# A transformer block on one core: when the turn of the softmax maxima and the copies of the scores are emitted

## The chip, the core and the metric

The kernel runs on one core of one Trainium2 chip. A core has a matrix engine (TensorE, PE in the profile; PEld are its weight loads), a vector engine (VectorE, DVE), a scalar engine for activations and copies (ScalarE, ACT), a general engine (GpSimd, POOL) and SyncE (SP), which issues most of the DMAs. Each has its own queue of instructions, and they wait for each other by semaphores. Matrix products end in PSUM, a small accumulation memory; all else lies in SBUF. The metric is the device time of one execution, in microseconds (us).

## What is computed

One block, float32 throughout: layer norm, attention with 32 heads of width 32, residual, layer norm, gated feed-forward network, residual, on x of shape (2, 1024, 1024).

```python
def _L0_attn_ref(x, attn_qkvw, attn_qkvb, attn_ow, attn_ob):
    qkv = x @ attn_qkvw + attn_qkvb
    ...
    scores = jnp.einsum('bhqd,bhkd->bhqk', q, k) * scale
    probs = jax.nn.softmax(scores, axis=-1)
    ctx = jnp.einsum('bhqk,bhkd->bhqd', probs, v)
    ctx = jnp.transpose(ctx, (0, 2, 1, 3)).reshape(B, S, H)
    return ctx @ attn_ow + attn_ob
...
    up = xt @ W_up.T
    gate = jax.nn.silu(xt @ W_gate.T)
    y = gate * up @ W_down.T
...
x = x + _L0_attn_ref(_layernorm(x, axis=-1), ...)
x = x + _L0_ffn_ref(_layernorm(x, axis=-1), ...)
```

W_gate and W_up are 2752 x 1024.

## The kernel before

**Units.** Attention is cut into 64 units: two batches, two blocks of 512 queries each, and 16 pairs of heads. Units are numbered 0 to 63 in that order; units 0 to 15 are the first phase. A unit has eight key tiles of 128 keys. The scores of one key tile, for both heads, are a PSUM tile `s` of 128 x 1024 (keys down, heads and queries across); there are two such tiles. `scores(i)` makes the key tiles 2i and 2i+1 with four small matmuls (L510). Each is then read twice: VectorE keeps a running maximum over the key tiles in `top` (L528), and ScalarE copies the scores to SBUF, `p` (L529). For key tile 0 VectorE copies it instead (L524), and the maximum of key tile 1 starts from that copy. Within `take`, which does both for one key tile, the maximum is emitted first and the copy right behind it.

**The maxima.** After key tile 7, `top` holds a maximum over eight keys for each partition and query, and it remains to take it over the 128 partitions. `maximum` does that in steps: VectorE transposes 32 x 32 blocks of half of `top` (L543) and reduces them into `part` (L544), the same for the other half, TensorE transposes `part` (L558, the instruction of `turn`, into one of the three PSUM tiles `lin` that all projections share), VectorE reduces once more, negated, to `neg` (L559). SyncE stores that in DRAM (L564) and loads it back spread over all partitions as `m` (L567).

**The exponentials.** `less_maximum` adds `m` to the copied scores (L574, on GpSimd; in the first phase key tiles 3 and 7 on VectorE), `exponential` is ScalarE's (L580), and `add` adds the exponentials of two key tiles (L590; on VectorE for key tiles 3 and 7, in the first phase for all four pairs, otherwise on GpSimd). `values` multiplies them with V, and their pair sums with ones for the softmax's divisor, into `acc` (L602). The copies live in a ring of `RING` buffers. The values of a unit lie in one of two buffers, which `load_v` fills by SyncE (L496).

**The rest.** The other work of TensorE is projections of q, k and v (L370, L432), the output projection (L764), gate and up products in a seven-product scheme (L906), and the down projection (L1047, L979). Their results leave the `lin` tiles by VectorE (L920 to L933, L1060, L776, L444) or ScalarE (L918, L384, L386).

**What sets the order.** The whole order is written out by an `Emitter`. It has a clock in ns, which advances by each step's cost in TensorE time (`MM4` = 855 for a full matmul of 512 columns). Steps come from two lists, a `fill` (projections and feed-forward) and a `paced` list (attention); the beats of the paced list are spread evenly over the cost of the list that they go with. There are eight beats to a unit, and even beats make scores. `later(delay, fn)` puts `fn` off until the clock has advanced by `delay`; when it is called, its instructions go to the end of their engines' queues. The numbers in the calls of `later` are thus places in the order, not times. `LAG` is the number of beats between the end of a unit's scores and its first `less_maximum`, beside a fixed eight; three beats later the values follow. `needs` and `gives` hold a step back until another is done in this clock, such as `("max", n)` for the subtractions of unit n.

Of the kernel before, what the change touches and what calls it, by code (L numbers as in the profile page):

```python
# [12 lines left out]
ALU = mybir.AluOpType  # L13
# [4 lines left out]
HD = 32  # L18
# [112 lines left out]
def preln_block_kernel(  # L131
# [14 lines left out]
    nc = tc.nc  # L146
# [13 lines left out]
    MM4, MM1 = 855.0, 230.0  # L160
    UNITS = HEADS // 2
    QTR = 4
    LAG = 2
    RUN = 4
    RING = NT + LAG + RUN + 4

# [27 lines left out]
    def Pt(name):  # L194
        return att.tile([P, S], F32, tag="p", bufs=RING, name=name)

    def lps(name, shape=(P, NH)):
        return psum.tile(list(shape), F32, tag="lin", bufs=3, name=name)

    def small(shape, tag, bufs, name):  # L200
        return const.tile(shape, F32, tag=tag, bufs=bufs, name=name)
# [27 lines left out]
    em = Emitter()  # L229
# [235 lines left out]
    class Unit:  # L465
# [35 lines left out]
        def scores(self, i):  # L501

            kts = (2 * i, 2 * i + 1)
            ps = [
                psum.tile([P, S], F32, tag="s", bufs=2, name=f"s_{self.name}_{kt}") for kt in kts
            ]
            for a in range(2):
                for h in range(2):
                    rows = slice((2 * a + h) * HD, (2 * a + h + 1) * HD)
                    nc.tensor.matmul(  # L510
                        ps[a][:, h * NH : (h + 1) * NH],
                        self.k[rows, i * P : (i + 1) * P],
                        self.q[rows, :],
                        start=True,
                        stop=True,
                    )


            for kt in kts:
                self.p[kt] = Pt(f"p_{self.name}_{kt}")  # L520

            def take(kt, s):
                if kt == 0:
                    nc.vector.tensor_copy(self.p[0], s)  # L524
                    return
                if kt == 1:
                    self.top = att.tile([P, S], F32, tag="top", bufs=1, name=f"top_{self.name}")
                nc.vector.tensor_tensor(self.top, s, self.p[0] if kt == 1 else self.top, ALU.max)  # L528
                nc.scalar.copy(self.p[kt], s)  # L529

            take(kts[0], ps[0])
            em.later(1700.0, lambda: take(kts[1], ps[1]))
            if kts[1] == NT - 1:
                self.maximum()

        def maximum(self):

            n = HD // NS
            self.m = att.tile([P, S], F32, tag="m", bufs=2, name=f"m_{self.name}")

            def half(s):
                cols = slice(s * NH, (s + 1) * NH)
                nc.vector.transpose(self.m[:, cols], self.top[:, cols])  # L543
                nc.vector.tensor_reduce(  # L544
                    part[:, s * n : (s + 1) * n],
                    self.m[:, cols].rearrange("p (b j) -> p b j", j=HD),
                    AX.X,
                    ALU.max,
                )

            for s in range(NS):
                em.later(4600.0 + 1800.0 * s, lambda s=s: half(s))
            d2 = dram.tile([S], F32, tag="d2", bufs=3, name=f"d2_{self.name}")
            neg = small([HD, HD], "neg", 1, f"neg_{self.name}")

            def turn():
                pt = lps(f"top_{self.name}", (P, P))
                nc.tensor.transpose(pt, part, ident)  # L558
                nc.vector.tensor_reduce(  # L559
                    neg, pt[:HD, :].rearrange("b (a i) -> b i a", i=HD), AX.X, ALU.max, negate=True  # L560
                )

            em.later(8600.0, turn)
            em.later(9600.0, lambda: nc.sync.dma_start(d2.rearrange("(b i) -> b i", i=HD), neg))  # L564
            em.later(
                12000.0,
                lambda: nc.sync.dma_start(self.m, d2.partition_broadcast(P)),  # L567
                ("max", self.n),
            )
# [62 lines left out]
    def attention_steps(cuts):  # L632
# [7 lines left out]
        def load_step(k, i):  # L640
            if k < len(units):
                q.add(lambda: units[k].load(i), needs=("qk", units[k].b, units[k].g))

        for i in range(2):
            load_step(0, i)
        for n in range(total + NT + LAG + 3):
            if n in cuts:
# [13 lines left out]
            else:  # L661
                q.add(lambda: None, beat=True)
            k, kt = divmod(n - NT - LAG, NT)
            if 0 <= k < len(units):
                if kt == 0:
                    q.add(units[k].differences)
                q.add(lambda k=k, kt=kt: units[k].less_maximum(kt), needs=("max", k))
            k, kt = divmod(n - NT - LAG - 3, NT)
            if 0 <= k < len(units) and kt % RUN == RUN - 1:
# [512 lines left out]
    with tc.manual_schedule():  # L1182
# [87 lines left out]
        keep = keep_qk  # L1270
        for (q, late), beats in zip(rests, [*lists[1:], None]):
            em.run(joined([keep, q]), beats, side=side)
            keep = late
# [53 lines left out]
```

## Time and profile before

| | |
|---|---|
| Median of 3 runs | 3360.42 us (3348.86 to 3375.26) |
| Profiled execution | 3347.63 us, span 3345.6 us |
| Mean granted clock of TensorE | 0.986 |
| Scores' first copy, L524 VectorE | 64 x 1223 ns |
| Scores' other copies, L529 ScalarE | 448 x 1012 ns |
| Maxima, L528 VectorE | 384 x 1222 ns, 64 x 1224 ns |
| Transposition and reduction of halves, L543, L544 | 128 x 701 ns, 128 x 686 ns |
| Transposition of `part`, L558 TensorE | 64 x 316 ns |
| Subtraction, L574 GpSimd | 480 x 2468 ns |
| Exponential, L580 ScalarE | 512 x 1057 ns |
| Addition of two exponentials, L590 | VectorE 160 x 1554 ns, GpSimd 96 x 2392 ns |

A line of the groups names the source line, the engine, what is written and read, shapes and count, then busy time, the mean of one, the idle time of the engine ahead of it, and what ended most of that. A line of the waits names who waited, for whom, then the total in us, the number of waits and the longest. In a timeline a row has its start and its length, the engine, line and operation, and in brackets the engine's idle time before it and what ended it. In the windows each engine's busy time is given with its number of instructions, then the granted clock of TensorE as a share of full speed, the DMA engines' share and GB/s.

### The profile page before, as it was taken

The numbers are of one execution on the slowest core, as the hardware profiler recorded it, in microseconds if no ns is written. First come the engines' busy times: TensorE is split into PE (matmuls) and PEld (weight loads), VectorE is DVE, ScalarE is ACT, GpSimd is POOL, SyncE is SP. The second block draws the span as 40 slices with busy tenths as digits, with TensorE's granted clock in tenths as the row PEclk, the third lists the DMA queues.
The fourth block names the chain that finished last, engine by engine and source line by source line (L and its number), as shares of the span: only waits on it lengthen the run. The fifth ranks groups of instructions, "written<-read, shape, count | busy, mean of one in ns | idle before, by whom it ended". The sixth has DMA issues, their size and how long they took to land.

```text
span 3345.6 us, 44180 instructions
## 1 busy us (share of the span) xinstructions
PE 3220.0 (96%) x16576; PEld 1819.2 (54%) x16576; DVE 1971.8 (59%) x2526; ACT 1375.1 (41%) x1506; POOL 1722.6 (51%) x839
## 2 busy tenths in 40 slices
PE   8999999999899999998999999989999999999999
PEld 4444444444346655663465556634655566476775
DVE  2366676664356666657566666665666664344434
ACT  2244554444355544453554545535544454010000
POOL 0267667775665555556755666567555555200000
PEclk9999999999999999999999999989999999999999
DMA  4566666663524454456344544463445444544552
GB/s 152 172 186 202 208 202 202 194 191 120 164 86 127 146 144 134 147 145 202 92 136 140 146 143 140 144 200 96 128 141 145 140 135 127 197 136 154 153 153 97
DMA packets 337251, 507.32 MB, mean 152 GB/s; under 512 B 105360, under 2 KB 122000, under 8 KB 337040
## 3 DMA queue, kind: packets, MB, share of 16 engines
q1 hardware_dynamic: 280848, 405.91, 40.1%
q10 hardware_dynamic: 56192, 98.60, 9.7%
q8 instruction: 132, 2.16, 0.3%
q14 instruction: 79, 0.65, 0.1%
HBM read 429.14 MB, written 75.24 MB: 151 GB/s over the span
## 4 chain that ended last, share of the span: by engine, by line
PE 81%; DVE 10%; DMA 3%; ACT 2%; issue 2%; POOL 1%; SPq 0%; ACTq 0%; DVEq 0%; POOLq 0%
PE p L906 27%; PE pq L370 11%; PE pd L1047 10%; PE acc L602 10%; PE s L510 7%; PE po L764 6%; PE pvv L432 6%; DVE top L528 2%; PE pd L979 1%; DVE x L1060 1%; DVE part L544 1%; DVE m L543 1%; DVE p L590 1%; PE pg L950 1%; POOL p L574 1%
## 5 line engine op out<-in xcount | busy, mean ns | idle before, releaser
L574 POOL TENSOR_TENSOR p<-p,m 128x1024 f32<-128x1024 f32 x480 | 1174.1, 2468 | 174.8 <-DMA m<-d 160.0
L529 ACT COPY p<-s 128x1024 f32<-128x1024 f32 x448 | 452.1, 1012 | 997.4 <-DVE top L528 959.6
L528 DVE TENSOR_TENSOR top<-s,top 128x1024 f32<-128x1024 f32 x384 | 469.1, 1222 | 397.1 <-PE s L510 380.6
L580 ACT ACTIVATE p<-p 128x1024 f32<-128x1024 f32 x512 | 530.4, 1057 | 262.3 <-POOL p L574 203.0
L906 PE MATMUL p<-sum,m 128*128 128x256 f32 x2688 | 616.3, 383 | 12.3 <-ACT gate L918 8.4
L906 PEld LDWEIGHTS p<-sum,m 128*128 128x128 f32 x2688 | 505.9, 191 | 120.2 <-issue 28.8
L590 POOL TENSOR_TENSOR p<-p,p 128x1024 f32<-128x1024 f32 x96 | 229.7, 2392 | 574.7 <-ACT p L580 568.1
L906 PE MATMUL p<-xn2T,m 128*128 128x256 f32 x2016 | 467.8, 383 | 3.7 <-ACT gate L918 2.8
L370 PE MATMUL pq<-xnT,wqk 128*128 128x512 f32 x1024 | 458.3, 600 | 0.1
L1047 PE MATMUL pd<-wp,h 128*128 128x512 f32 x960 | 432.3, 599 | 2.5 <-DVE x L1060 2.3
L906 PEld LDWEIGHTS p<-xn2T,m 128*128 128x128 f32 x2016 | 379.6, 191 | 84.8 <-issue 27.3
L370 PEld LDWEIGHTS pq<-xnT,wqk 128*128 128x128 f32 x1024 | 190.1, 191 | 249.8 <-issue 246.2
L1047 PEld LDWEIGHTS pd<-wp,h 128*128 128x128 f32 x960 | 178.8, 190 | 231.3 <-issue 204.7
L510 PE MATMUL s<-q,k 32*128 32x512 f32 x2048 | 301.7, 660 | 0.0
L1060 DVE TENSOR_TENSOR x<-pd,x 128x512 f32<-128x512 f32 x360 | 236.7, 683 | 78.9 <-PE pd L1047 78.7
L602 PE MATMUL acc<-p,vals 128*32 128x256 f32 x4096 | 280.0, 392 | 0.0
L590 DVE TENSOR_TENSOR p<-p,p 128x1024 f32<-128x1024 f32 x160 | 248.7, 1554 | 31.0 <-ACT p L580 30.9
L1158 POOL TENSOR_TENSOR ws<-raw 128x512 f32<-128x512 f32 x62 | 95.3, 1537 | 315.6 <-DMA raw<-in_w_gu 201.3
L432 PE MATMUL pvv<-wv,xnT 128*128 128x512 f32 x512 | 229.4, 597 | 0.7 <-DVE vv L444 0.7
L764 PE MATMUL po<-wo,ctx 128*128 128x512 f32 x512 | 228.4, 599 | 0.0
L602 PEld LDWEIGHTS acc<-p,vals 128*32 128x32 f32 x4096 | 122.4, 112 | 174.0 <-issue 103.2
L969 POOL MEMSET h<- 64x512 f32 x4 | 2.1, 518 | 339.4 <-PE pd L1047 339.4
(96 smaller groups left out, 2597.6 us busy)
## 6 DMA issues: line engine op xcount, KB each, us to landing
m<-dws SPq DMA_DIRECT2D x336, 256.0 KB
m<-in_w_gu SPq DMA_DIRECT2D x252, 256.0 KB
wp<-ddn SPq DMA_DIRECT2D x160, 256.0 KB
m<-d SPq DMA_DIRECT2D x64, 512.0 KB
wp<-in_w_dn SPq DMA_DIRECT2D x120, 256.0 KB
raw<-in_w_gu ACTq DMA_DIRECT2D x84, 256.0 KB
dws<-ws ACTq DMA_DIRECT2D x84, 256.0 KB
x<-in_x SPq DMA_DIRECT2D x32, 512.0 KB
```

Source lines behind the costliest of these rows:

```text
L370: nc.tensor.matmul(ps, wqk[b, g, w, hk][:, k, :], xnT[b, s][:, kc, :], start=(kc == 0), stop=(kc == KC - 1),)
L432: nc.tensor.matmul(st["ps"], xnT[b, t // TB][:, kc, (t % TB) * P : (t % TB + 1) * P], st["w"][kc], start=(kc == 0), stop=(kc == KC - 1),)
L510: nc.tensor.matmul(ps[a][:, h * NH : (h + 1) * NH], self.k[rows, i * P : (i + 1) * P], self.q[rows, :], start=True, stop=True,)
L528: nc.vector.tensor_tensor(self.top, s, self.p[0] if kt == 1 else self.top, ALU.max)
L529: nc.scalar.copy(self.p[kt], s)
L574: eng.tensor_tensor(p, p, self.m, ALU.add)
L580: nc.scalar.activation(self.p[kt], self.p[kt], AF.Exp, scale=SCALE)
L590: eng.tensor_tensor(self.p[kt], self.p[kt], self.p[kt - 1], ALU.add)
L602: nc.tensor.matmul(self.acc[j * HD : (j + 1) * HD, c : c + NQ], w(h), self.p[kt][:, q0 : q0 + NQ], start=start, stop=stop, skip_group_chec ...
L764: nc.tensor.matmul(st["ps"], ctxT[b, blk][:, g, t * P : (t + 1) * P], st["w"][hf, g], start=(g == 0), stop=(g == G - 1),)
L906: nc.tensor.matmul(ps, mats[c, n][:, kc, :], rhs, start=(kc == 0), stop=(kc == hk - 1),)
L1047: nc.tensor.matmul(st["pd"], lefts[n](pi)[:, j, t * P : (t + 1) * P], st["wp", pi, n, j], start=(j == 0), stop=(j == PART // 2 - 1),)
```

## The change

Four things are altered, all in the class `Unit` and its constants.

1. `LAG` is 3 instead of 2, and with it the ring of score buffers has one more.
2. The first key tile's scores are copied by ScalarE, not VectorE. The maximum of key tile 1 still starts from that copy.
3. The maximum and the copy of a key tile are separate functions, and the copy is emitted further back: for a pair's first tile at 1600 (before: at once, behind the maximum), for its second at 3300 (before: 1700). For a unit's first pair, the copy of key tile 0 comes at once, the maximum of key tile 1 at 2600 (before: 1700), and its copy at 4200 (before: 1700).
4. `turn` is emitted at 10,500 (before: 8600), the store of the maxima at 12,000 (9600), and their broadcast at 14,500 (12,000).

What is computed is the same, and so are the number and the shapes of all matmuls, DMAs and other instructions, but for the 64 copies that change engine. The change adds six lines, so that line numbers after the class's `scores` are six higher (L558 becomes L564, L590 L596, L602 L608, L906 L912); the maxima move from L528 to L526.

```diff
-    LAG = 2
+    LAG = 3
...
-            def take(kt, s):
-                if kt == 0:
-                    nc.vector.tensor_copy(self.p[0], s)
-                    return
+            def largest(kt, s):
                 if kt == 1:
                     self.top = att.tile([P, S], F32, tag="top", bufs=1, name=f"top_{self.name}")
-                nc.vector.tensor_tensor(self.top, s, self.p[0] if kt == 1 else self.top, ALU.max)
+                if kt > 0:
+                    nc.vector.tensor_tensor(self.top, s, self.p[0] if kt == 1 else self.top, ALU.max)
+
+            def keep(kt, s):
                 nc.scalar.copy(self.p[kt], s)
 
-            take(kts[0], ps[0])
-            em.later(1700.0, lambda: take(kts[1], ps[1]))
+            if i == 0:
+                keep(0, ps[0])
+                em.later(2600.0, lambda: largest(1, ps[1]))
+            else:
+                largest(kts[0], ps[0])
+                em.later(1600.0, lambda: keep(kts[0], ps[0]))
+                em.later(1700.0, lambda: largest(kts[1], ps[1]))
+            em.later(3300.0 if i > 0 else 4200.0, lambda: keep(kts[1], ps[1]))
             if kts[1] == NT - 1:
                 self.maximum()
...
-            em.later(8600.0, turn)
-            em.later(9600.0, lambda: nc.sync.dma_start(d2.rearrange("(b i) -> b i", i=HD), neg))
+            em.later(10500.0, turn)
+            em.later(12000.0, lambda: nc.sync.dma_start(d2.rearrange("(b i) -> b i", i=HD), neg))
             em.later(
-                12000.0,
+                14500.0,
                 lambda: nc.sync.dma_start(self.m, d2.partition_broadcast(P)),
                 ("max", self.n),
             )
```

## The prediction

> **What bounds the kernel now.** I read the page first, then who waited for whom on TensorE, then the groups kept apart by shape, then VectorE's timeline around the worst stalls, and last the windows with the granted clock. The page's first part and its chain of waits:
>
> ```profile
> PE 3220.0 (96%) x16576; PEld 1819.2 (54%) x16576; DVE 1971.8 (59%) x2526; ACT 1375.1 (41%) x1506; POOL 1722.6 (51%) x839
> ...
> PE 81%; DVE 10%; DMA 3%; ACT 2%; issue 2%; POOL 1%; SPq 0%; ACTq 0%; DVEq 0%; POOLq 0%
> ```
>
> TensorE is the bound: it stands still for only 3345.6 - 3220.0 = 125.6 us. No edit removes a matmul, so all that can change is this idle time and the clock. The waits of TensorE alone (total, times, longest):
>
> ```profile
> PE top L558 <- DVE part L544: 64.2, 26, 11.0
> PE pd L979 <- DVE x L1060: 13.1, 3, 6.5
> PE p L906 <- ACT gate L918: 11.2, 8, 4.0
> PE pt_a L258 <- ACT x L247: 11.0, 4, 7.8
> ```
>
> Over half of the idle time is one instruction: the transposition of the column maxima (`turn`, L558) is reached before VectorE has reduced them (`part`, L544). Three more waits before L558 (3.5, 2.5, 1.9) make it 72.1 us in 29 units of 64. Going through the 64 transpositions, six of these stalls are long (unit 7: 3.46; 19: 10.96; 21: 4.47; 34: 5.21; 50: 5.62; 62: 3.79; together 33.5) and the other 23 are 0.73 to 2.75 us (38.6). VectorE's timeline ahead of the longest:
>
> ```profile
> 898.84 2.55 DVE L528 TENSOR_TENSOR top<-s,top 128x1024 f32<-128x1024 f32 x2 [7.45 <-PE s L510]
> 907.53 2.26 DVE L590 TENSOR_TENSOR p<-p,p 128x1024 f32<-128x1024 f32 x1 [6.14 <-ACT p L580]
> 909.72 0.70 DVE L543 STREAM_TRANSPOSE m<-top 128x512 f32<-128x512 f32 x1
> ...
> 911.79 0.69 DVE L544 TENSOR_REDUCE part<-m 128x16 f32<-128x512 f32 x1
> ```
>
> The maxima were complete at 901.39. VectorE then waited 6.14 us for an exponential, because the addition of two exponentials (L590) of the unit before stands ahead of the four steps that TensorE needs. In the order of work this addition (key tile 3) stands just ahead of those steps in all 63 units that have one.
>
> **A later turn.** At `LAG` 3 and 10,500 the turn moves, in the two programs' order of instructions, behind two more full matmuls in 60 units of 64; in the others it moves 2.14 us (unit 21), 0.86 (50), 1.29 (62) and 0 (34). A full matmul is 0.859 us (the chain shows 32 records, two to a matmul, in 13.74 us), so TensorE arrives 1.71 us later with work that it had to do anyway.
>
> **A beat more of lag.** Moving subtraction, exponential and addition back by one beat puts that addition behind the four steps and ahead of `neg` (L559) in all 63 units. The groups with shapes kept apart:
>
> ```profile
> L529 ACT COPY p<-s 128x1024 f32<-128x1024 f32 x448 | 452.1, 1012 | 997.4 <-DVE top L528 959.6 <-DVE up L928 4.6 <-DMA ddn<-ws 4.4
> ...
> L590 DVE TENSOR_TENSOR p<-p,p 128x1024 f32<-128x1024 f32 x160 | 248.7, 1554 | 31.0 <-ACT p L580 30.9
> ...
> L524 DVE COPY p<-s 128x1024 f32<-128x1024 f32 x64 | 78.2, 1223 | 58.2 <-PE s L510 57.8
> ```
>
> The addition takes 1.22 us alone and 1.55 in the mean, so a late VectorE reaches `part` at least 1.2 us earlier: 1.71 + 1.22 = 2.93, more than each of the 23 short stalls, and I count them gone, but for unit 8. Of the long ones there remain, with the addition's own time taken from each timeline: unit 19: 10.96 - 1.71 - (6.14 + 2.26) = 0.9; 21: 4.47 - 2.14 - 1.16 = 1.2; 34: 5.21 - 2.58 = 2.6; 50: 5.62 - 0.86 - 3.27 = 1.5; 62: 3.79 - 1.29 - 1.22 = 1.3. In the first 16 units VectorE also does the subtraction of key tile 3 (2.29 us, L574), which the lag moves to the wrong side: units 7 and 8 keep 3.46 - 1.71 + 1.07 = 2.8 and 2.45 - 1.71 + 1.07 = 1.8; the other 14 arrive 0.4 to 3.4 us early today and stay hidden. Left are 12.1 us; the term is **-60 us** (-40 if the addition in front costs nothing, -72 at most).
>
> The lag's other orders: the attention's last matmul keeps its place, because the last list holds one beat less, so the tail is not longer. SyncE's load of the values (L496) had 0.9 to 1.7 us of matmuls between the last reader of its buffer and itself, and now has none; it waits up to 1.7 us more a unit, with weight loads queued behind it. It waited 22.95 us at 916.7 without any stall of TensorE on weights, so I count 0.
>
> **What the turn sends on.** `neg` follows the turn, so the store of the maxima (L564) and their broadcast (L567) come 2.4 and 2.5 us later in the emission's clock; the subtraction that waits for them comes a beat (some 5 us) later. Their cover grows by 2.5 us, and GpSimd's 160.0 us of waits on that broadcast (40 times) should fall. GpSimd holds TensorE for only 4.5 us, so this brings about 0. `neg` now stands behind an addition that may wait for an exponential, and until it has run one of the three `lin` banks is held; two tiles of gate and up work (4 matmuls of 0.43 us each) cover 2 x 1.71 = 3.4 us. Beyond that it would cost time: 0 to 5 us, taken as 1.
>
> **The first copy on ScalarE.** 64 copies of 1.223 us leave VectorE (-78.2 us busy), 64 of 1.012 come to ScalarE (+64.8, 41% to 43% busy). Neither engine is the bound; alone worth 0. The added wait is that VectorE's first maximum needs this copy, and what is queued behind it on VectorE are the reads that empty `lin`. Against VectorE's start of the copy today, ScalarE had finished all earlier work before it in 53 of the 64 units; the latest are 5.34 (unit 7), 2.21 and 2.06, and 1.44 at most outside the first 16 units. The maximum is emitted 2.6 us behind the copy and the copy takes 1.0, so ScalarE may be 1.6 late for nothing, and 3.4 more under the cover above. Between 0 and 6 us; taken as 0.
>
> **Copies behind the maxima.** They come 1.6 us later in the order (2.5 for a unit's first pair). ScalarE waits 959.6 us on VectorE's maxima in these copies, so this lets the exponentials and the gate copies go first, which can give back part of the 11.2 us (L906 <- L918). Against it, a score buffer is held longer: the copies end 4.8 us after the scores in the median, and the next scores come 10.0 after. In five of 255 cases the margin is under 1.6 (0.3, 0.8, 1.2, 1.3, 1.5): 1.6 x 5 - 5.1 = 2.9 us, and 0.9 more for the first pair's 2.5. Taken as +4, with no gain.
>
> **The clock.** Windows of 20 us around three of the stalls (the number ahead of the last two is the granted clock):
>
> ```profile
> 900.00:920.00 20.00, 9.04 (x65) 3.46 (x64) 8.89 (x10) 6.24 (x7) 19.09 (x9) 0.74 0.72 249
> 1215.00:1235.00 20.00, 18.11 (x104) 10.05 (x104) 11.52 (x17) 4.41 (x5) 10.95 (x6) 0.91 0.43 127
> 1565.00:1585.00 20.00, 14.79 (x84) 5.79 (x83) 11.33 (x12) 6.06 (x7) 10.22 (x6) 0.83 0.77 274
> ```
>
> Eleven stalls before L558 are followed by such a drop: one window at 0.74, five at 0.83, five at 0.91, which is 20 x (0.26 + 5 x 0.17 + 5 x 0.09) = 31 us of clock. Part of it lies inside the stall and is counted already; I keep 20 and take three quarters of that, **-15 us** (bounds 0 and -25). The second window holds a stall of only 1.89 us. The Trainium skill, page "TensorE: Matmul & The Clock Gate", section "What's actually happening", says that the array falls to half clock after an idle window of about 3.4 us. By that rule the short stalls would cost no clock and the term would be about half, -7; the trace disagrees, with drops behind stalls of 1.89, 2.15, 2.38, 2.68 and 2.75 us.
>
> **Sum.** -60 - 15 + 1 + 4 = -70. The profiled execution took 3347.6 us (span 3345.6), so 3277.6 on its scale. The median of the runs is 12.8 us above it, so 3290 there. I put 3285, between the two.
>
> **Rivals.** First, the stall moves: VectorE's backlog is real work, and when TensorE no longer stops at L558 it stops at the next `lin` tile instead. For it: VectorE is 68% busy in the gate and up stretches, and without gaps ahead of many of the stalls. Against it: the lateness there is 2.75 us or less in the 23 short cases, inside the 3.4 us cover. If two thirds come back, 60 + 15 shrinks to 25 and the 5 stays: 3328 to 3341, within 1%. Chance 0.2.
>
> Second, slower: the first maximum is caught behind ScalarE. VectorE works its queue in order (the 6.14 us above), and ScalarE waits for GpSimd's subtractions 203.0 us in 74 exponentials, the longest 11.2. If a unit's first copy lands behind such a wait, VectorE stops, then `lin`, then TensorE. It decides from the point where ScalarE is more than 1.6 + 3.4 = 5.0 us late at that copy. At 8 us late in each of 64 units it costs 64 x 3 = 192 - 70 = +122: 3470 us; even with a third of the units it would be +60 - 70, no change. Only one unit is past 5.0 today. Chance 0.13, because the lag also reorders GpSimd around the changes of block, which I can't read from before. The Trainium skill, page "PSUM — Partial Sum Buffer", section "Engine vs sequencer instructions", says the same of these queues, that they are strictly first in, first out.
>
> Third, more gain than counted: the waits at L906 and L979 (24.3 us) share the late VectorE and go too: 3277.6 - 24.3 = 3253, or 3266 on the scale of the median. Chance 0.1. The forecast itself, 3266 to 3325, has 0.57.
>
> **How the numbers follow.** A measurement of this kernel can tell about 1% (33 us; its three runs lie 26 us apart). Faster by more than that is the forecast and the third rival, 0.67; within it the first rival, 0.2; slower the second, 0.13. The range of 3245 to 3360 takes in the forecast, the first rival and the third, with some 10 us on both sides for the bounds of the clock and of the later turn, and leaves out the second.
>
> **What would show it.** In the profile after, TensorE's wait on `part` should be under 15 us and its busy time about the same with a span some 70 shorter; L590 should stand behind L544 on VectorE; the clock should be 0.99 or more; ScalarE's wait on the maxima should fall well below 959.6. I would be wrong if a new wait of TensorE on `lin` readers (L906, L1047, L764) or on scores (L510) of more than 20 us appears, or if VectorE's first maximum waits for L529 by more than 5 us in many units.

## The result and the profile after

| | before | after |
|---|---|---|
| Median of 4 runs each | 3357.03 us (3348.86 to 3375.26) | 3321.23 us (3316.05 to 3326.36) |
| Ratio, 95% interval | 1 | 0.9886 [0.9842, 0.993] |
| Profiled execution, span | 3347.63, 3345.6 us | 3320.48, 3318.7 us |
| TensorE busy, idle | 3220.0, 125.6 us | 3231.4, 87.3 us |
| Granted clock | 0.986 | 0.993 |

The kernel became faster by 1.1%, and by 1.3% when it was measured again (0.9866 [0.9834, 0.9898], below). The forecast was 3285, a gain of 70 us on the scale of the profiled execution; this execution gained 27. The page after, its first part and the engines' shares in its chain of waits:

```profile
PE 3231.4 (97%) x16576; PEld 1807.2 (54%) x16576; DVE 1904.9 (57%) x2462; ACT 1431.9 (43%) x1570; POOL 1704.9 (51%) x839
...
PE 27%; DVE 1%; DMA 0%; ACT 0%; issue 0%; SPq 0%; DVEq 0%
```

The chain was followed only over the last part of the span this time (its shares add up to 28%), so it says little. The first number says more: TensorE is busy for 11.4 us **longer** than before, with the same 16576 matmul records and a better clock. The idle time fell by 38.3 us, so 38.3 - 11.4 = 26.9 us of the span are gone. A second profiled execution of the changed kernel has a span of 3319.4 us, busy 3241.2, idle 78.2 and a clock of 0.989. TensorE's waits after (total, times, longest):

```profile
PE top L564 <- DVE part L550: 13.0, 7, 3.2
PE pd L1053 <- DVE x L1066: 11.5, 13, 4.6
PE s L510 <- ACT p L529: 11.2, 5, 4.4
```

The wait that the change aimed at fell from 64.2 to 13.0 us; with the small waits ahead of the same instruction it is 18.8 (13.0, and 2.7, 2.0, 0.7 and 0.4 on other releasers) after 72.1. Two waits have grown: the down projection on VectorE's reading of its tile (2.3 to 11.5), and the scores on ScalarE's copies (none to 11.2).

Unit 19 had the longest stall before, 10.96 us. VectorE's timeline around the same place (start, length, engine, line, operation; in brackets its idle time before it):

```profile
901.52 2.55 DVE L526 TENSOR_TENSOR top<-s,top 128x1024 f32<-128x1024 f32 x2 [7.65 <-PE s L510]
904.16 0.71 DVE L549 STREAM_TRANSPOSE m<-top 128x512 f32<-128x512 f32 x1
...
906.25 0.69 DVE L550 TENSOR_REDUCE part<-m 128x16 f32<-128x512 f32 x1
911.69 2.28 DVE L596 TENSOR_TENSOR p<-p,p 128x1024 f32<-128x1024 f32 x1 [4.76 <-ACT p L586]
913.89 0.27 DVE L565 TENSOR_REDUCE neg<-top 32x32 f32<-32x128 f32 x1
```

The reductions now end at 906.94, directly behind the maxima, and the addition (L590, now L596) with its 4.76 us of waiting stands behind them. TensorE's timeline there:

```profile
904.09 1.02 PE L770 MATMUL po<-wo,ctx 128*128 128x512 f32 x2
908.00 1.13 PE L510 MATMUL s<-q,k 32*128 32x512 f32 x4 [2.88 <-ACT p L529]
909.49 1.64 PE L510 MATMUL s<-q,k 32*128 32x512 f32 x4 [0.36 <-ACT p L529]
911.06 0.47 PE L564 MATMUL top<-ident,part 128*128 128x128 f32 x1
911.32 4.63 PE L770 MATMUL po<-wo,ctx 128*128 128x512 f32 x8
```

L564 waits for nothing. But 3.24 us of the 10.96 have come back a few instructions ahead of it, at the scores: both score buffers are still held by ScalarE's copies. Two groups that answer to those of before (busy, mean ns of one, idle time before them and what ended most of it):

```profile
L529 ACT COPY p<-s 128x1024 f32<-128x1024 f32 x512 | 516.6, 1012 | 908.1 <-DVE top L526 682.8
...
L596 DVE TENSOR_TENSOR p<-p,p 128x1024 f32<-128x1024 f32 x160 | 273.0, 1706 | 121.7 <-ACT p L586 121.5
```

ScalarE's wait on the maxima fell from 959.6 to 682.8 us, while VectorE's wait on exponentials, in front of its additions, rose from 30.9 to 121.5.

### The profile page after: what moved, and what is told of

Same layout as the page of the kernel before. It is cut to its first block, busy times and chain, and to the rows that moved or that the text cites. A ratio compares the mean times of both kernels' runs of the same rounds, so it can differ in the third digit from the quotient of the medians.

```text
span 3318.7 us, 44204 instructions
## 1 busy us (share of the span) xinstructions
PE 3231.4 (97%) x16576; PEld 1807.2 (54%) x16576; DVE 1904.9 (57%) x2462; ACT 1431.9 (43%) x1570; POOL 1704.9 (51%) x839
## 5 line engine op out<-in xcount | busy, mean ns | idle before, releaser
L580 POOL TENSOR_TENSOR p<-p,m 128x1024 f32<-128x1024 f32 x480 | 1172.0, 2464 | 27.3 <-DMA m<-d 27.2
L529 ACT COPY p<-s 128x1024 f32<-128x1024 f32 x512 | 516.6, 1012 | 908.1 <-DVE top L526 682.8
L526 DVE TENSOR_TENSOR top<-s,top 128x1024 f32<-128x1024 f32 x384 | 468.3, 1220 | 318.7 <-PE s L510 308.6
L912 PE MATMUL p<-sum,m 128*128 128x256 f32 x2688 | 619.7, 383 | 11.6 <-DVE gate L928 6.8
L586 ACT ACTIVATE p<-p 128x1024 f32<-128x1024 f32 x512 | 531.0, 1057 | 194.3 <-POOL p L580 177.7
L596 POOL TENSOR_TENSOR p<-p,p 128x1024 f32<-128x1024 f32 x96 | 227.6, 2371 | 678.7 <-ACT p L586 644.7
L912 PEld LDWEIGHTS p<-sum,m 128*128 128x128 f32 x2688 | 503.4, 190 | 133.2 <-issue 43.0
L912 PE MATMUL p<-xn2T,m 128*128 128x256 f32 x2016 | 473.1, 383 | 2.2 <-ACT gate L924 1.3
L370 PE MATMUL pq<-xnT,wqk 128*128 128x512 f32 x1024 | 465.2, 602 | 0.0
L1053 PE MATMUL pd<-wp,h 128*128 128x512 f32 x960 | 440.8, 605 | 11.4 <-DVE x L1066 10.9
L912 PEld LDWEIGHTS p<-xn2T,m 128*128 128x128 f32 x2016 | 377.6, 191 | 99.1 <-issue 45.1
L596 DVE TENSOR_TENSOR p<-p,p 128x1024 f32<-128x1024 f32 x160 | 273.0, 1706 | 121.7 <-ACT p L586 121.5
L1053 PEld LDWEIGHTS pd<-wp,h 128*128 128x128 f32 x960 | 178.3, 192 | 245.2 <-issue 207.0
L510 PE MATMUL s<-q,k 32*128 32x512 f32 x2048 | 298.6, 642 | 11.2 <-ACT p L529 11.2
L608 PE MATMUL acc<-p,vals 128*32 128x256 f32 x4096 | 271.4, 382 | 3.5 <-DVE p L596 3.5
L1164 POOL TENSOR_TENSOR ws<-raw 128x512 f32<-128x512 f32 x62 | 88.5, 1428 | 337.7 <-DMA raw<-in_w_gu 184.1
L608 PEld LDWEIGHTS acc<-p,vals 128*32 128x32 f32 x4096 | 119.8, 109 | 145.0 <-issue 71.2
```

The source lines that it names most:

```text
L370: nc.tensor.matmul(ps, wqk[b, g, w, hk][:, k, :], xnT[b, s][:, kc, :], start=(kc == 0), stop=(kc == KC - 1),)
L510: nc.tensor.matmul(ps[a][:, h * NH : (h + 1) * NH], self.k[rows, i * P : (i + 1) * P], self.q[rows, :], start=True, stop=True,)
L580: eng.tensor_tensor(p, p, self.m, ALU.add)
L586: nc.scalar.activation(self.p[kt], self.p[kt], AF.Exp, scale=SCALE)
L596: eng.tensor_tensor(self.p[kt], self.p[kt], self.p[kt - 1], ALU.add)
L608: nc.tensor.matmul(self.acc[j * HD : (j + 1) * HD, c : c + NQ], w(h), self.p[kt][:, q0 : q0 + NQ], start=start, stop=stop, skip_group_chec ...
```

## The experiments

No kernel leaves out work. Each ratio is against the kernel before, on the same chip, with its 95% interval. The profiled execution of a kernel can lie 17 us from its median, so a trace is used to see where waits stand, and the ratios to compare kernels. Two questions are tested: where the longer busy time of TensorE comes from, and what each part of the change is worth.

**The values one beat later, in the kernel before.** The values (`acc`, L602) follow the first `less_maximum` by three beats. With `LAG` 2 they fall in an even beat, directly behind that beat's scores; with 3 they fall in an odd one, among full matmuls. My theory was that this costs TensorE time at the changes between small-tile and full matmuls; the rival was that the busy time grew for another reason. The edit makes that move alone:

```diff
-    RING = NT + LAG + RUN + 4
+    RING = NT + LAG + RUN + 5
...
-        for n in range(total + NT + LAG + 3):
+        for n in range(total + NT + LAG + 4):
...
-            k, kt = divmod(n - NT - LAG - 3, NT)
+            k, kt = divmod(n - NT - LAG - 4, NT)
```

> The kernel before, with the values' matmuls (acc) one beat later and one more score buffer; nothing else. Theory A (a block of acc matmuls of its own, between full matmuls, costs TensorE about 0.2 us, which a block right behind the scores does not): 123 blocks leave the scores, so 123 x 0.2 = +24 us against before, 3381, with TensorE's listed waits as before (about 120 us). Theory B (the part of the gain that is missing went into new waits on VectorE and ScalarE; where the acc blocks stand costs nothing): within 10 us of before, 3347 to 3367.

Measured: 1.0044 [1.0013, 1.0076], 15 us slower. The kernel before, TensorE's timeline:

```profile
1499.96 1.07 PE L602 MATMUL acc<-p,vals 128*32 128x256 f32 x16
...
1502.69 3.70 PE L950 MATMUL pg<-xn2T,m 128*128 128x512 f32 x8
1506.23 3.60 PE L1047 MATMUL pd<-wp,h 128*128 128x512 f32 x8
1509.75 1.14 PE L510 MATMUL s<-q,k 32*128 32x512 f32 x8
```

The same stretch of the experiment:

```profile
1504.99 3.70 PE L950 MATMUL pg<-xn2T,m 128*128 128x512 f32 x8
1508.53 1.02 PE L1047 MATMUL pd<-wp,h 128*128 128x512 f32 x2
1509.48 1.07 PE L602 MATMUL acc<-p,vals 128*32 128x256 f32 x16
...
1512.21 2.84 PE L1047 MATMUL pd<-wp,h 128*128 128x512 f32 x6
1514.98 1.14 PE L510 MATMUL s<-q,k 32*128 32x512 f32 x8
```

Here one has to read starts, not lengths (the rows overlap). The eight L1047 records of before take 1509.75 - 1506.23 = 3.52 us. Cut into two and six by the values they take (1509.48 - 1508.53) + (1514.98 - 1512.21) = 0.95 + 2.77 = 3.72, so 0.20 more. The values themselves take 2.73 in both (1502.69 - 1499.96, 1512.21 - 1509.48). Over all records, leaving out half-clock time, the first small-tile matmul behind full ones starts 0.094 us late and the second full matmul behind a small-tile block 0.102 late. A block that stands directly behind another pays these once for both. Counted in program order, 123 of the 128 blocks of values stood behind scores before; in this experiment and in the changed kernel none does: 123 x (0.094 + 0.102) = 24.1 us, no part of which appears as a wait. The ratio gives 15 us, and its interval 4 to 26, which holds the 24 and does not by itself exclude the 10 that the rival allowed. The trace decides: TensorE is busy for 3248.3 us, 28.3 more than before at the same granted clock (0.986), while its idle time is 128.3 us after 125.6.

**The values beside the scores again, in the changed kernel.** They come a further beat later, ahead of the even beat's scores (and `load_v` behind the scores):

```diff
-            if n < total and kt % 2 == 0:
-                q.add(lambda k=k, i=kt // 2: units[k].scores(i), MM4, beat=True)
-            else:
-                q.add(lambda: None, beat=True)
+            q.add(lambda: None, beat=True)
+            k, kt = divmod(n - NT - LAG - 4, NT)
+            ...
+                    q.add(lambda k=k, v=v: units[k].values(v), cost)
+            k, kt = divmod(n, NT)
+            if n < total and kt % 2 == 0:
+                q.add(lambda k=k, i=kt // 2: units[k].scores(i), MM4)
+            if n < total and kt == NT - 2:
+                q.add(units[k].load_v, needs=("v", units[k].b, units[k].hf))
...
-            k, kt = divmod(n - NT - LAG - 3, NT)
```

> The changed kernel, with the values' matmuls one beat later still, directly ahead of the scores of an even beat, so that acc and scores stand side by side again. Theory A: the 24 us come back, about 3297 (ratio to before 0.982), with the wait at the transposition of the maxima still under 20 us. Theory B: no change against the changed kernel, 3321 (0.989); its waits on VectorE and ScalarE stay.

Measured: 0.9842 [0.9809, 0.9875], and in a second run:

> The changed kernel with acc ahead of the scores of an even beat, once more: 0.9842 of before was measured (0.981 to 0.9875). Theory A: under the changed kernel's 0.9866 to 0.9886 again, since 21 us of TensorE's time at the change of tile shape are gone by the trace. Theory B: equal to it.

0.986 [0.9828, 0.9892]. The changed kernel has 0.9886 [0.9842, 0.993] and 0.9866 [0.9834, 0.9898], so the mean of two is better by 0.25%, where 24 us would be 0.7%, and the intervals overlap: a gain is not shown. In the records the changes of shape are back at the cost of before (260 entries to small tiles, as many returns). Part of what took the rest back stands in the waits of its TensorE:

```profile
PE pd L1053 <- DVE x L1066: 20.0, 20, 4.6
PE pd L985 <- DVE x L996: 13.8, 3, 6.4
```

In the changed kernel 11.5 and 3.0 us were spent there. In all, TensorE is idle for 95.8 and 95.1 us in the two profiled executions, after 87.3 and 78.2 in the changed kernel's two. The other part shows in no list of waits: matmuls start later than usual while the record before them still runs. Added up from the distances between starts, outside half-clock time, that is 33 and 29 us here, 17 and 14 there. On the means of the two executions 13 and 15 us are lost again, more than the 24 that came back. That TensorE, without those 24 us, reaches the backlog of VectorE and ScalarE earlier would explain it, but no run tests that.

**The later turn alone, in the kernel before.**

```diff
-            em.later(8600.0, turn)
-            em.later(9600.0, ...)
+            em.later(10500.0, turn)
+            em.later(12000.0, ...)
             em.later(
-                12000.0,
+                14500.0,
```

> The kernel before with the turn, the store and the broadcast of the maxima at 10500, 12000 and 14500; nothing else. Theory A: the wait for part falls from 72 to about 33 us, and with 10 us of clock the time falls by 35 to 50: 3307 to 3322, as fast as the whole change. Theory B: the wait moves to the next lin tile and at most half is kept: 3335 or more.

Measured: 0.9935 [0.9899, 0.9971], 22 us faster, between the two theories. TensorE's wait on `part` falls to 24.0 us (15 times), all stalls ahead of L558 to 25.8, while those at the down projection grow from 15.7 to 30.8.

**The beat of lag alone, in the kernel before.**

```diff
-    LAG = 2
+    LAG = 3
```

> The kernel before with LAG 3 and nothing else: the addition of key tile 3 moves behind the reduction of the maxima, and the acc blocks leave the scores. Theory A: TensorE's wait for part falls from 72 to about 34 us by the addition's place alone (1.22 us or more a unit), with some 10 us of clock, and 24 us are lost again at the acc blocks: 20 to 25 us faster than before, ratio 0.993. Theory B (what counts is the waits alone): 45 to 50 us faster, ratio 0.986. Theory C (the addition's place is nothing, the later turn is all): slower than before by the 15 us that the run with the acc blocks moved alone has shown, ratio 1.004.

Measured: 1.0024 [0.9998, 1.0051], no gain. TensorE's waits, and VectorE's on the exponentials:

```profile
PE top L558 <- DVE part L544: 52.7, 23, 5.2
```

```profile
DVE p L590 <- ACT p L580: 129.1, 47, 7.9
```

I had looked for 34 us in the first row, and by its ratio the run stands nearest to the third theory. The addition's place did change, but the gain at L558 is 11.5 us only, and the shape of the values takes 24.1 the other way. VectorE's wait for exponentials is four times that of before, with the same emission delays. Why was not taken apart; it is the lag that brings it, since the later turn alone leaves it at 39.4 us.

**The change without its beat of lag**, `LAG` 2 and all else as changed:

```diff
-    LAG = 3
+    LAG = 2
```

> The changed kernel with LAG 2: later turn and later copies, but the addition of key tile 3 ahead of the reduction again, and the acc blocks behind the scores in 111 units' cases. Theory A: TensorE's wait for part rises from 19 to about 33 us (the 72 of before less 1.71 a unit) and some 8 us of clock with it, while about 13 to 24 us come back from the acc blocks: 3315 to 3330. Theory B: only the waits count: 3321 + 22 = 3343.

Measured: 0.9925 [0.9892, 0.9957]. **The same with the addition moved by its own delay**, so that it stands behind the reductions without the lag:

```diff
-    LAG = 3
+    LAG = 2
...
-                em.later(8100.0, lambda: self.add(kt), ("added", self.n, kt))
+                em.later(11600.0 if kt == 3 else 8100.0, lambda: self.add(kt), ("added", self.n, kt))
```

> The changed kernel with LAG 2, and the addition of key tile 3 emitted at 11600 instead of 8100, so that it stands behind the reduction while the acc blocks stay behind the scores. Theory A: both gains at once, TensorE's wait for part under 20 us and 12 to 24 us from the acc blocks: 10 to 20 us faster than the changed kernel on the same chip. Rival: the values now wait for the late addition (3.4 us of cover in the order of work), and TensorE's wait at acc rises above 15 us, which takes the gain back.

Measured: 0.9906 [0.9869, 0.9943], not told apart from the row above. Its TensorE waits:

```profile
PE acc L608 <- DVE p L596: 20.2, 10, 8.3
...
PE top L564 <- DVE part L550: 10.1, 7, 3.5
```

The addition behind the reductions is what the stall at L564 needs (10.1 us is left here, 35.5 with the addition in front, there in the longest of ten executions; the later turn alone, with the addition in front, leaves 24.0), but at `LAG` 2 it is then too near to the values that read its sum: 20.2 us. The beat of lag gives that room (3.5 us in the changed kernel), and `LAG` 3 pays for it with the place of the values. What the beat is worth within the change is not told apart: 0.9925 without it, 0.9886 and 0.9866 with it, and the intervals overlap.

**The change without the copies.** `take` is as before, the lag and the turn as changed:

```diff
-            if i == 0:
-                keep(0, ps[0])
-                em.later(2600.0, lambda: largest(1, ps[1]))
-            ...
-            em.later(3300.0 if i > 0 else 4200.0, lambda: keep(kts[1], ps[1]))
+            take(kts[0], ps[0])
+            em.later(1700.0, lambda: take(kts[1], ps[1]))
```

> The changed kernel with the copies and maxima emitted as before (first copy on VectorE, each copy right behind its maximum). Theory A: the copies are worth nothing: within 0.3% of the changed kernel on the same chip; TensorE's wait at the scores for ScalarE's copies (11 us) falls to under 3 and VectorE's later reads of lin tiles take about as much back. Rival: the copies behind the maxima are what lets the gate copies and exponentials through; without them the change loses 10 us or more, ratio 0.992 or above.

**The changed kernel again**, on the same chip:

> The changed kernel itself, for a comparison on the same chip: 0.9886 of before, interval 0.984 to 0.993.

Measured: 0.9993 [0.9972, 1.0014] without the copies, 0.9866 [0.9834, 0.9898] with them. So the part that I had priced at +4 us carries the whole gain that is left once the lag has been paid for. A stretch of VectorE's timeline without the copies:

```profile
2159.27 0.69 DVE L544 TENSOR_REDUCE part<-m 128x16 f32<-128x512 f32 x1
...
2160.98 4.31 DVE L936 TENSOR_TENSOR h<-gate,up 128x512 f32<-128x512 f32 x1 [0.69 <-ACT gate L934]
2165.22 1.21 DVE L590 TENSOR_TENSOR p<-p,p 128x1024 f32<-128x1024 f32 x1
2166.35 1.21 DVE L524 COPY p<-s 128x1024 f32<-128x1024 f32 x1
2167.49 0.27 DVE L559 TENSOR_REDUCE neg<-top 32x32 f32<-32x128 f32 x1
```

and TensorE's at its end:

```profile
2167.81 1.13 PE L906 MATMUL p<-sum,m 128*128 128x256 f32 x4 [1.64 <-DVE neg L559]
```

The later turn puts `neg` behind the next unit's first copy. In program order L524 stands between the reductions and `neg` in 61 units here and in 1 unit before. Until `neg` has run, one of the three `lin` banks is held, and the matmul at 2167.81 waits 1.64 us for it; 1.21 of that is the copy. (L936, ahead of both, lasts 4.31 us here and 1.24 in the mean, and delays `neg` too.)

That order alone is not the cause. It stands in the same 61 units in the run with the later turn alone, which is faster than before and has no wait of TensorE on `neg`. Here too these waits are small, 3.9 us ahead of L906 and 0.6 ahead of L1047, where the profiled executions with the copies are 31 us shorter:

```profile
PE p L906 <- ACT gate L918: 7.0, 5, 2.4
...
PE p L906 <- DVE neg L559: 3.9, 5, 1.6
```

**Each half of the copies by itself**, with lag and turn as changed. First, the first copy on ScalarE, the others right behind their maxima:

```diff
-                em.later(2600.0, lambda: largest(1, ps[1]))
+                em.later(2600.0, lambda: both(1, ps[1]))
             else:
-                largest(kts[0], ps[0])
-                em.later(1600.0, lambda: keep(kts[0], ps[0]))
-                em.later(1700.0, lambda: largest(kts[1], ps[1]))
-            em.later(3300.0 if i > 0 else 4200.0, lambda: keep(kts[1], ps[1]))
+                both(kts[0], ps[0])
+                em.later(1700.0, lambda: both(kts[1], ps[1]))
```

(`both` is `largest` and then `keep`.)

> The changed kernel with only the first copy moved to ScalarE; every other copy is emitted right behind its maximum, as before. Theory A2 (after the later turn, the first copy on VectorE would stand between the reduction and neg in 61 units, 1.2 us in front of neg and of the reads that empty lin; moving it away is what the copies' part is worth): as fast as the changed kernel, 0.985 to 0.991 of before. Rival (the later emission of the other copies, which lets ScalarE do gate copies and exponentials first, is what counts): about 0.997 to 1.0, like the kernel without the copies' part.

Then the first copy on VectorE, the others late:

```diff
             if i == 0:
-                keep(0, ps[0])
-                em.later(2600.0, lambda: largest(1, ps[1]))
+                nc.vector.tensor_copy(self.p[0], ps[0])
             else:
                 ...
-                em.later(1700.0, lambda: largest(kts[1], ps[1]))
-            em.later(3300.0 if i > 0 else 4200.0, lambda: keep(kts[1], ps[1]))
+            em.later(1700.0, lambda: largest(kts[1], ps[1]))
+            em.later(3300.0, lambda: keep(kts[1], ps[1]))
```

> The changed kernel with the first copy on VectorE as before, and the other copies emitted behind the maxima as in the change. Theory A2: 0.996 to 1.0 of before, as without the copies' part. Rival: 0.985 to 0.991.

Measured: 0.991 [0.988, 0.994] for the first copy alone, 0.9926 [0.9896, 0.9955] for the late copies alone. With neither 0.9993, with both 0.9866 (on another chip): each half brings 0.7 to 0.8%, and together 1.3%. I had expected one of the two to bring nothing. The traces give each half a few us of its own. The waits of L906 on the gate copies are 7.0 us with neither, 8.5 with the first copy alone, 0.8 with the late copies alone, 1.3 and 0.8 in the changed kernel's two executions: these the late copies remove. The waits on `neg` are 4.5 with neither, 0.7 with the first copy alone, 1.8 with the late copies alone (where L524 again stands ahead of `neg` in 61 units), 0.3 and 0.0 with both: these the first copy removes, and the late copies in part. Together that is some 10 of the 31 us. The copies without the later turn and the lag were not run.

**A faster version.** In the kernel with the values beside the scores, VectorE's reciprocals of the softmax sums stand in its queue before their DMA has landed. Their group there, and the edit that emits them later:

```profile
L696 DVE RECIPROCAL recs<-sums 128x32 f32<-128x32 f32 x16 | 5.6, 348 | 23.3 <-DMA sums<-dsum 23.3
```

```diff
-            em.later(7000.0, go, ("rec", b, blk, i))
+            em.later(10000.0, go, ("rec", b, blk, i))
```

> The changed kernel with acc ahead of the scores of an even beat (as in the run e2), and the reciprocals of the softmax's divisors emitted at 10000 instead of 7000, so that VectorE does not stop for the load of the sums (2.2 and 7.9 us in e2). Theory: VectorE's waits on that load go, and TensorE's waits behind them (4.6 and 4.4 us): 5 to 9 us under e2, 0.982 of before. Rival: the load of the context that follows 3 us later makes the block's first output products wait: no gain, or slower than e2.

The same group:

```profile
L696 DVE RECIPROCAL recs<-sums 128x32 f32<-128x32 f32 x16 | 5.3, 333 | 3.3 <-DMA sums<-dsum 3.3
```

Measured: 0.9802 [0.9769, 0.9836], median 3301.07 us. The wait on the DMA went from 23.3 to 3.3 us, and TensorE's at L1053 from 20.0 (22.7 in the second run) to 16.5. Against the kernel that it is made from (0.986 on the same chip) the intervals overlap a little, but each of its six executions (to 3314.45 us) is shorter than each of the other's six (from 3316.34). The changed kernel's two ratios were measured on other chips; the interval here ends just below that of the first (from 0.9842) and just touches that of the second (from 0.9834).

## Why the prediction was right, and where it was wrong

The sign and the range held, and the stall that the prediction named is the one that went. But half of the gain did not come, and that a gain is left at all owes something to luck: with the later turn and the lag, the two steps that carried the sum, there is none without the copies (0.9993; the lag takes back what the turn alone brings, 0.9935), and the sum had the copies at a loss. The terms, against the traces of the changed kernel's two profiled executions:

| Step | put at | found | found again |
|---|---|---|---|
| Stalls ahead of L558, all causes | -60 (72.1 to 12.1) | -53.3 (to 18.8) | -52.6 (to 19.5) |
| Clock, outside the stalls | -15 | -17.2 | -3.9 |
| `neg` and `lin`, copies | +1, +4 | other stalls +15.0 together | +5.2 |
| "The lag's other orders" | 0 | +24.1 | +24.1 |
| Left over in the busy time | not in the sum | +4.5 | +1.0 |
| Sum | -70 | -26.9 | -26.2 |

The third column is worked out as follows. The idle time fell by 38.3 us, and 53.3 of that is at L558, so the others grew by 15.0. Busy time rose by 11.4. The shape of the values took 24.1. TensorE worked at half clock for 72.4 us before and 37.9 after, and half of the difference is -17.2. The 4.5 left over are matmuls that start late while the record before them still runs. The fourth column is made the same way, with 64.5 us of work at half clock and with a busy time 21.2 longer and an idle time 47.4 shorter than before. The stalls ahead of L558 agree between the two executions; the clock and the other stalls differ by 13 and 10 us, so no single trace sizes those.

**A later turn, a beat more of lag.** Right in kind and nearly in size: 13.0 us on `part` (under 15 was asked for), L590 behind L544 in all 63 units, as in unit 19. Apart from each other the two steps did not work as added: the turn alone gave 0.9935, the lag alone 1.0024 with 52.7 us still at L558. The sum gave the turn 40 of its 60 us and the addition's place 20. The turn alone takes all stalls ahead of L558 from 72.1 to 25.8, 46.3 us; with the lag beside it (without the copies) they are 18.6, so the addition's place was worth 7 there. The step that took the addition's own time off each stall saw where its wait for the exponential would go, but not that this wait would grow from 30.9 to 121.5 us.

**The lag's other orders.** This is the step that failed most. It went through the last beat and the loads of V, and missed that `values` stands at `LAG` + 3 beats: an odd lag takes it out of the beats that make scores. It costs 24.1 us in the trace, and 15 (4 to 26) measured when it is done alone. I had said that busy time would stay "about the same"; +11.4 with a better clock was the sign that showed it.

**The first copy on ScalarE ("alone worth 0") and the copies behind the maxima ("taken as +4, with no gain").** Wrong. I looked for what the new wait could cost and priced the 78.2 us that leave VectorE at nothing, since VectorE is not the bound; and I named the gate copies that late copies let go first, but counted no gain for them. Without the copies there is no gain at all (0.9993); each half brings 0.7 to 0.8%. The traces show the waits on the gate copies and on `neg` going, some 10 us; for the rest the cause is open. The cost that I feared is there too: scores wait 11.2 and 6.3 us for ScalarE in the two executions, where I had put 3.8. But they wait 11.7 without the copies as well, so it is not shown that the copies bring it.

**The clock.** Put at 0.99 or more; it is 0.993 in the profiled execution and 0.988 to 0.993 in all ten of the changed kernel, where the kernel before shows 0.979 to 0.988. The time lost to half clock, in all, is 0.014 x 3345.6 = 47 us before and 0.007 x 3318.7 = 23 after. Of these 24 us 17 fell on working matmuls, near the 15 that I had kept; in the second execution it is only 3.9.

**GpSimd.** The 160.0 us on the broadcast fell to 27.2, and that was worth as little as said: the wait of ScalarE on GpSimd only went from 203.0 to 177.7.

**The rivals.** The first one (the stall moves) happened in part: 15.0 us of the 53.3 came back (5.2 of 52.6 in the second execution), at the down projection and the scores, not two thirds. Of the second (the first maximum behind ScalarE) there is hardly a trace: those 64 maxima wait 7.7 us in total for L529. (At `LAG` 2, with all else as changed, they wait 37.0.) The third did not come: the waits at L906 and L979, all releasers together, went from 29.3 to 21.3 us, but L1047 (now L1053) took 9.2 more.

Still open: why VectorE waits so much more for exponentials at `LAG` 3, and why the two halves of the copies each bring over half of their gain alone, of which the waits named above are only a third.

## What to carry to other kernels

Where one number sets the place of several steps, go through every step that hangs on it, and ask beside which instructions it lands: an odd lag cost 24 us of TensorE's time here, where the change brought 27 in the same trace. Do not price load that leaves an engine at nothing because that engine is not the bound: the two halves of the copies were put at 0 and +4 us, and without them the rest of the change brought nothing. Parts of a change need not add up: run the change without each of them. Time lost between matmuls of different shapes shows in no list of waits; add up the distances between starts, or ask why busy time grew with the same work.

## What the hardware showed that was not expected

- A change from full to small-tile matmuls (32 rows or 32 columns) delays the first small one by 0.094 us in the mean of the records, and the second full one behind the block by 0.102 us; two small-tile kinds next to each other (scores, values) pay it once. One block alone: 0.20 us; the 123 blocks that moved: 24 us.
- Half clock can follow short stalls. In the timeline of unit 19 after, the granted clock falls to half at 909.98 for 3.41 us, behind a stall of 2.88 us and one of 0.36: four records of scores take 1.64 us, where the four before them took 1.13, and L564 takes 0.47 where the same transposition takes 0.27 in the run without the copies. The Trainium skill, page "TensorE: Matmul & The Clock Gate", section "What's actually happening", puts the fall at an idle window of about 3.4 us; this trace shows it below that. It need not come: a stall of 2.96 us that ended at 941.69 has none behind it.
- VectorE's additions of exponentials last 1554 ns in the mean before, 1706 after and 1966 in the change with `LAG` 2 (1996 with the addition moved there), where the one in the timeline without the copies takes 1.21 us: where an instruction stands in the order changed its duration too. What it then ran beside was not tried.
